# One copy fewer of the attention product, and three steps of the end re-ordered, in a kernel of two gated blocks

## The chip, the cores and the metric

The kernel runs on one core of one Trainium2 chip. The metric is the device time of one execution in microseconds (us). The profile shows one such execution: what each engine did and when. The engines are named as in the profile: PE multiplies matrices, PEld is its weight load, DVE is the vector engine, ACT the scalar engine, POOL the GpSimd engine, and SP issues most DMAs (SPq is its queue).

## The reference

The input x has 4 batches of 1024 rows of 512 numbers. Two layers follow one another. Each normalises x, computes an attention `s` and a feed-forward network `g` from the same normalised x, and adds their gated product:

```
xn = layernorm(x); s = attention0(xn); g = silu(ffn0(xn)); x = x + s * g
xn = layernorm(x); s = attention1(xn); g = silu(ffn1(xn)); x = x + s * g
```

Layer 0 has a linear attention with decay and a ternary-weight FFN; the change does not touch them. Attention 1 is a softmax attention with 16 heads of 32: `q`, `k` and `v` are projections, `q` and `k` are rotated by position, `y = softmax(q k^T / sqrt(32)) v`, and the output is `y wo^T`. FFN 1 has weights in whole numbers from 0 to 63 with the zero point 128 and a scale for each row: `W = (wq - 128) * s`.

## The kernel before

The kernel is one program with five parts in order: attention 0 (to 624 us), FFN 0 (to 1160 us), attention 1 (to 2598 us), FFN 1 (to the end), and a check of FFN 1's weights with a fallback that does not run here. The order of the work on PE is written out by hand. On the other engines a planner chooses the order by its own estimates, except that instructions marked with `keep_in_program_order` (below: pinned) keep the order in which the program names them. Each engine carries out its own queue in order and waits there for what an instruction needs; SP's queue of DMA issues does so too. A tile comes from a pool by its tag, with a fixed number of buffers, and a new tile waits until everyone who read the old one in its buffer is done.

**Units and steps.** Attention 1 is cut into 32 units: batch b (4), group g of four heads (4), and half `qh` of the queries (2), in this order. A unit has 512 queries and 8 key blocks of 128. The loop over `s` (L1177) has 8 steps for a unit, and steps 256 to 268 to finish. Step `s` holds work of several units:

- `top`: the scores `sq` of queries by keys for unit s // 8, of which DVE takes the maxima (L1079). After the eighth step `turn_max` sends the maxima through memory to `mT`.
- `exps(e)` with e = s - 12: scores `sk` of keys by queries (L1105), less the maximum (L1111), and on ACT their exponentials `pT` (L1116, two instructions; three buffers). Exponential e is key block kb = e % 8 of unit e // 8. Then `part` adds up the exponentials over the key blocks: on POOL (L1143 the first addition of a unit, L1145 the others), and on DVE from step 256 on.
- `weigh(e - 1)`: PE adds `v` times `pT` to `y` (L1124). After the last key block ACT copies `y` to `yr` (L1284).
- half a chain of matmuls, where one is waiting: `heads_in` projects q, k and v of a later group (L866; ACT copies to `raw`, DMAs swap rows to `rr`, and POOL rotates in L924 and L925), and `wo_out` multiplies four finished groups with `wo` (L866 too) once the last is divided.

**The division.** The sums over the keys of a unit are taken on DVE: `sums_of` (L967, L972) eight times, two in a step; `gather` (L980 to L984) writes them out and loads them turned, into `sides`, which has the one buffer of the tag that the transposes of `sums_of` use; `invert` (L993, L998) takes the reciprocal, writes it to `inverse_d` (L1001) and loads it spread over the partitions, as `zs` (L1009, four DMAs); `times` (L1017) multiplies `yr` by `zs` on POOL and writes `yT`, which `wo_out` reads. Counted by `i` from the unit's first sums, these are steps 0 to 3, 4, 7 and 10. Unit 30 has steps of its own, written out for the end of the loop; unit 31 is summed on PE and divided in `divide` after it. `yr` has two buffers; `yT` has five for `qh = 0` and six for `qh = 1`.

**Weights.** In steps 244 to 255 SP loads one weight of FFN 1 in each (`weight`, L777, 256 KB, to a tile of the tag `raw`, which has three buffers), and ACT subtracts 128 (L790) one step later, in `loaded()`. Both are pinned. The last two conversions are both named in step 255. The rest of the weights follow in FFN 1.

After the loop PE does the output chains of units 30 and 31 and goes on to FFN 1.

Of the kernel before, what the change touches and what calls it, by code (L numbers as in the profile page):

```python
# [12 lines left out]
F32 = mybir.dt.float32  # L13
# [3 lines left out]
ALU = mybir.AluOpType  # L17
AX = mybir.AxisListType

P = 128  # L20
# [15 lines left out]
def kernel(ctx, tc, ins, out):  # L36
    nc = tc.nc
# [48 lines left out]
    w0 = es1.enter_context(tc.tile_pool(name="w0", bufs=1, reuse_waits="tile"))  # L86
# [159 lines left out]
    with ExitStack() as es:  # L246
# [4 lines left out]
        p2 = es.enter_context(tc.tile_pool(name="a0", bufs=2, reuse_waits="tile"))  # L251
# [273 lines left out]
        for n, (blk, g) in enumerate(steps):  # L525
# [10 lines left out]
            nxt = None  # L536
            if n + 1 < len(steps):
                nxt = project(*steps[n + 1])
# [31 lines left out]
    with ExitStack() as es:  # L570
# [3 lines left out]
        p2 = es.enter_context(tc.tile_pool(name="f0", bufs=2, reuse_waits="tile"))  # L574
# [193 lines left out]
    def weight(stage, pool, pinned=False):  # L768

        m = len(ws)  # L770
        n, c = needed[m]
        q = stage(f"{n}_int{c}").bitcast(I32).rearrange("p (k n) -> p k n", n=P)
        if n == "down":
            src = ins["wq_downT"][c * P : (c + 1) * P, :].rearrange("p (k n) -> p k n", n=P)
        else:
            src = ins[f"wq_{n}T"][:, c * P : (c + 1) * P].rearrange("(k p) n -> p k n", p=P)
        load = nc.sync.dma_start(out=q, in_=src)  # L777
        j = m // 4
        if j not in fours:
            tag = quads[j] if j < len(quads) else f"wf{j}"  # L780
            fours[j] = pool.tile([P, KD, D], F32, tag=tag, name=f"wf{j}")
        w = ws[n, c] = fours[j][:, m % 4, :].bitcast(F32R).rearrange("p (k n) -> p k n", n=P)
        if pinned:
            tc.keep_in_program_order(load)

        def less():
            if pinned:

                tc.keep_in_program_order(
                    nc.scalar.activation(w, q, AF.Identity, bias=less128)  # L790
                )
            else:
                nc.vector.tensor_scalar(w, q, -128.0, None, ALU.add)

        return less
# [19 lines left out]
    with ExitStack() as es:  # L815
# [9 lines left out]
        TB = N // P  # L825
# [187 lines left out]

        def times(u, yr):
            b, g, qh = units[u]
            yT = p2.tile([P, 512], F32, tag=f"yT{qh}", name=f"yT_{b}_{g}_{qh}", bufs=5 + qh)
            tc.keep_in_program_order(nc.gpsimd.tensor_tensor(yT, yr, zss.pop(u), ALU.mult))  # L1017
            yTs[b][g, qh] = yT

        def divide(u, yr, z):  # L1020

            b, g, qh = u
            zs = p2.tile([P, 512], F32, tag="mT", name=f"zs_{b}_{g}_{qh}")
            nc.scalar.copy(zs, z)
            yT = p2.tile([P, 512], F32, tag=f"yT{qh}", name=f"yT_{b}_{g}_{qh}", bufs=5 + qh)
            for c in range(TPB):
                cols = slice(c * P, (c + 1) * P)
                nc.vector.reciprocal(zs[:, cols], zs[:, cols])
            nc.gpsimd.tensor_tensor(yT, yr, zs, ALU.mult)
            yTs[b][g, qh] = yT  # L1030

        def wo_out(b, qh, yT, bank):
            def chain(i):
# [92 lines left out]
                    start=(kb == 0), stop=(kb == TB - 1),  # L1126
                )

        loaded = None

        def exps(e):
            if not 0 <= e < TB * nu:
# [44 lines left out]
        for s in range(TB * nu + LAG + 1):  # L1177

            e = s - LAG
            if s % (2 * TB) == 0 and s < TB * nu:

                assert not must
                n = s // (2 * TB) + 1
                if n < 4 * B:
                    b, g = divmod(n, 4)

                    two = (nc.sync, nc.gpsimd) if s == 0 else (nc.sync, nc.sync)  # L1190
                    must.extend(
                        heads_in(
                            b, g, acc1, {(w, h): two for w in ("wk", "wq") for h in range(2)}
                        )
                    )
                    if g == 3 and b + 1 < B:
                        load1(b + 1)

                left = 2 if n < 4 * B else TB
            if s in soon and s < TB * nu:  # L1200
                spare.extend(wo_out(*soon.pop(s), acc1))
            if s % 2 == 0:

                chain = None
                if spare and left and s < TB * nu:
                    chain = spare.popleft()
                    left -= 1
                elif must:
                    chain = must.popleft()
            if s == 2 * TB:  # L1210
                W["wo"] = shared_tile("wo", "wo")
                tc.keep_in_program_order(
                    nc.sync.dma_start(
                        out=W["wo"], in_=ins["woT"].rearrange("(k p) n -> p k n", p=P)
                    )
                )
            if s % 4 == 0 and s // 4 < TPB:
                lates[s + 2] = s // 4, late(s // 4)
            if s < TB * nu:
                u, j = divmod(s, TB)  # L1220
                if j == 0:
                    mx[u] = p2.tile([P, TPB, 4, 2], F32, tag="mx", name=f"mx_{u}")
                for pair in range(2):
                    top(u, j, pair, mx[u])
                if j == TB - 1:
                    m2 = twice[u % 2][:, :, :8].rearrange("p q (h c) -> p q h c", c=2)

                    w = p2.tile([P, TPB, 4, 2], F32, tag="m1", name=f"m1_{u}")
                    nc.vector.tensor_reduce(
                        w[:, :, :, 0], mx.pop(u), AX.X, ALU.max, negate=True  # L1230
                    )
                    for out, sign in ((w[:, :, :, 1], -1.0), (m2[:, :, :, 0], 1.0)):
                        nc.scalar.activation(
                            out.bitcast(F32R), w[:, :, :, 0], AF.Copy, scale=sign
                        )
                    nc.vector.tensor_reduce(m2[:, :, :, 1], w, AX.X, ALU.add)

            zu, at = divmod(s - 3 * TB, TB)
            for u, i in ((zu - 1, at + TB), (zu, at)):
                if 0 <= u < nu - 2:  # L1240
                    if i < 4:
                        for c in (2 * i, 2 * i + 1):
                            sums_of(u, parts[u], c)
                        if i == 3:
                            parts.pop(u)
                    elif i == 4:
                        gather(u)
                    elif i == 7:
                        invert(u)
                    elif i == 10:  # L1250
                        times(u, ys.pop(u))
                        b, g, qh = units[u]
                        if g == 3:
                            soon[s + 2] = b, qh, yTs[b]

            u = nu - 2
            if s == TB * nu + 7:
                for c in range(8):
                    sums_of(u, parts[u], c)
                parts.pop(u)  # L1260
            elif s == TB * nu + 8:
                gather(u)
            elif s == TB * nu + 10:
                invert(u)
            elif s == TB * nu + LAG:
                times(u, ys.pop(u))
                soon[s] = units[u][0], units[u][2], yTs[B - 1]
            late_exp = s >= TB * nu
            if late_exp:
                exps(e)  # L1270
            if 1 <= e <= TB * nu:
                u, kb = divmod(e - 1, TB)
                if kb == 0:
                    ys[u] = pp.tile([P, 512], F32, tag="y", name=f"y_{u}")
                weigh(u, kb, pTs[e - 1], ys[u])
                if u == nu - 1 and kb < TB // 2:

                    if kb == 0:
                        z_last = acc1(f"z_{u}")
                    total(z_last, pTs[e - 1], kb, TB)  # L1280
                pTs.pop(e - 2, None)
                if kb == TB - 1:
                    yr = p2.tile([P, 512], F32, tag="yr", name=f"yr_{u}")
                    nc.scalar.copy(yr, ys[u])  # L1284
                    ys[u] = yr
            held = 0
            if s % TB == 0 and 0 < s <= TB * nu:
                turn_max(s // TB - 1)
            if s in lates:
                late_turn(*lates.pop(s))  # L1290
            else:
                held = 1
                advance(1)
            if not late_exp:
                exps(e)
            advance(4 - held)
            if TB * nu - 12 <= s < TB * nu:

                nxt = weight(raw1, w0, True)
                if loaded:  # L1300
                    loaded()
                loaded = nxt
                if s == TB * nu - 1:
                    loaded()

        soon = [*soon.values()]
        for new in soon:
# [306 lines left out]
```

## Time and profile before

| | |
|---|---|
| time, median of 3 runs | 3091.44 us (3087.67, 3091.44, 3104.02) |
| the profiled execution | 3092.4 us, of which the span of its instructions is 3090.6 us |
| mean granted TensorE clock | 0.992 |
| busy, share of the span | PE 98%, PEld 56%, DVE 62%, POOL 51%, ACT 37% |
| attention 1 (1160.6 to 2598.3 us) | PE 1411.0, POOL 1171.0, DVE 923.7, ACT 597.8 us busy of 1437.7 |
| last FFN (2598.3 us to the end) | PE 479.1 us busy of 492.3 |
| exponentials, L1116 | 512 instructions, 1021 ns each |
| additions to `part` on POOL, L1145 and L1143 | 182 of 4545 ns and 31 of 4538 ns |
| copy of y, L1284 (ACT) | 32 of 585 ns |
| product with the reciprocal, L1017 (POOL) | 31, median 1272 ns |

The busy times count matmuls from their start to a modelled end, so a busy PE may still be held up. A wait is shown as the idle time before an instruction together with the instruction that ended it, as far as the semaphores show it. PEclk is the granted TensorE clock, 1.00 at full speed. In a step with projections PE needs 5.2 to 5.8 us, without them 4.6 us, as the starts of the y matmuls (L1124) in the timeline show.

### The profile page before, as it was taken

Reading aid. Unit: us, or ns where it says so; the run is one execution under the profiler, and the core shown is the slowest. Engines: PE = TensorE matmul, PEld = TensorE weight load, DVE = VectorE, ACT = ScalarE, POOL = GpSimd, SP = SyncE. Lnnn points to the kernel's source line nnn. Section 1 sums busy time; section 2 is a strip of 40 time slices with the busy share of each in tenths; the row PEclk is TensorE's granted clock in tenths of the full one; section 3 lists DMA queues with packets and bytes.
Section 4 is the critical chain, followed back from the end, with each engine's and each line's share of the span. In section 5 each row is a group of like instructions: output and inputs, shape, how many; then the busy total and the mean of one; then the engine's idle time right before and its main releaser. Section 6 shows DMA issues by size and latency. Waiting matters only on the chain.

```text
span 3090.6 us, 61333 instructions
## 1 busy us (share of the span) xinstructions
PE 3029.4 (98%) x25681; PEld 1725.8 (56%) x25681; DVE 1931.0 (62%) x3038; ACT 1155.4 (37%) x1677; POOL 1570.5 (51%) x745
## 2 busy tenths in 40 slices
PE   9999999999999998999999999999999999999998
PEld 5555555578778873333334444433344425888886
DVE  4444555467777776576666666666666665566655
ACT  3111111145556542444444444444444453333332
POOL 1221212234444444888898988988898960001001
PEclk9999999999999998999999999999999999999999
DMA  4232222323223231010001000010000114222111
GB/s 137 86 86 86 86 86 72 127 96 100 95 92 109 96 129 52 10 45 17 18 21 47 23 21 22 21 52 23 23 20 24 26 55 152 89 69 75 59 52 56
DMA packets 131150, 197.25 MB, mean 64 GB/s; under 512 B 33200, under 2 KB 47024, under 8 KB 130736
## 3 DMA queue, kind: packets, MB, share of 16 engines
q1 hardware_dynamic: 123456, 171.72, 18.7%
q0 software_dynamic: 7280, 21.39, 1.9%
q8 instruction: 203, 3.33, 0.5%
q14 instruction: 83, 0.68, 0.1%
q10 hardware_dynamic: 128, 0.13, 0.0%
HBM read 124.25 MB, written 60.53 MB: 60 GB/s over the span
## 4 chain that ended last, share of the span: by engine, by line
PE 54%; POOL 2%; ACT 1%; SPq 1%; issue 1%; DMA 1%; DVE 1%; POOLq 0%; ACTq 0%; DVEq 0%
PE sk L1105 9%; PE sq L1075 8%; PE y L1124 7%; PE gate L1347 5%; PE up L1347 5%; PE dn L1369 5%; PE wo L866 4%; PE wk L866 3%; PE v1ps L866 3%; PE wq L866 3%; PE sk L1111 2%; ACT pT L1116 1%; POOL part L1145 1%; SPq L920 1%; POOL rr L924 0%
## 5 line engine op out<-in xcount | busy, mean ns | idle before, releaser
L1145 POOL TENSOR_TENSOR part<-part,pT 128x2048 f32<-128x2048 f32 x182 | 827.2, 4545 | 31.2 <-ACT pT L1116 23.3
L1079 DVE TENSOR_REDUCE mx<-sq 128x2 f32<-128x1024 f32 x512 | 605.4, 1219 | 367.8 <-PE sq L1075 367.3
L1116 ACT ACTIVATE pT<-sk 128x1024 f32<-128x1024 f32 x512 | 495.9, 1021 | 610.4 <-PE sk L1111 592.7
L1075 PE MATMUL sq<-wkT,wqT 32*128 32x512 f32 x2048 | 331.0, 642 | 13.9 <-ACT pT L1116 11.2
L1105 PE MATMUL sk<-wqT,wkT 32*128 32x512 f32 x2048 | 332.5, 649 | 4.1 <-ACT pT L1116 3.7
L1124 PE MATMUL y<-pT,v 128*32 128x512 f32 x2048 | 278.7, 615 | 0.1
L1391 POOL TENSOR_TENSOR th<-th,x 128x512 f32<-128x512 f32 x31 | 40.1, 1293 | 458.0 <-DVE th L1390 379.0
L646 PE MATMUL pj<-wpj,hp 128*128 128x512 f32 x1024 | 262.3, 395 | 3.8 <-DVE hp L606 3.8
L593 PE MATMUL fc<-xp,wfc 128*128 128x512 f32 x1024 | 259.0, 395 | 3.6 <-ACT h L598 2.9
L614 POOL TENSOR_TENSOR sums<-sums,h 128x512 f32<-128x512 f32 x112 | 160.6, 1434 | 197.8 <-ACT h L598 192.6
L1111 PE MATMUL sk<-mT,onesr 2*128 2x512 f32 x1024 | 244.5, 799 | 0.0
L382 PE MATMUL qk<-xnT,wqkv 128*128 128x512 f32 x512 | 228.7, 599 | 0.7 <-ACT xnT L156 0.7
L646 PEld LDWEIGHTS pj<-wpj,hp 128*128 128x128 f32 x1024 | 190.8, 188 | 52.5 <-DVE hp L606 11.1
L593 PEld LDWEIGHTS fc<-xp,wfc 128*128 128x128 f32 x1024 | 189.2, 188 | 47.5 <-ACT h L598 6.1
L606 DVE TENSOR_TENSOR hp<-h,hp 128x512 fp32r<-128x512 f32 x128 | 129.2, 1009 | 85.6 <-ACT hp L603 85.6
L1105 PEld LDWEIGHTS sk<-wqT,wkT 32*128 32x128 f32 x2048 | 100.0, 185 | 134.4 <-issue 106.6
L1347 PE MATMUL gate<-xp,wf 128*128 128x512 f32 x704 | 174.1, 389 | 0.0
L1347 PE MATMUL up<-xp,wf 128*128 128x512 f32 x704 | 173.9, 389 | 0.0
L1369 PE MATMUL dn<-wf,hp 128*128 128x512 f32 x704 | 173.5, 389 | 0.0
L1143 POOL TENSOR_TENSOR part<-pT,pT 128x2048 f32<-128x2048 f32 x31 | 140.7, 4538 | 63.7 <-ACT pT L1116 63.6
L1075 PEld LDWEIGHTS sq<-wkT,wqT 32*128 32x128 f32 x2048 | 93.0, 184 | 132.9 <-issue 42.7
L382 PEld LDWEIGHTS qk<-xnT,wqkv 128*128 128x128 f32 x512 | 94.8, 190 | 112.0 <-issue 103.5
(236 smaller groups left out, 4454.6 us busy)
## 6 DMA issues: line engine op xcount, KB each, us to landing
s<-s SPq DMA_DIRECT2D x96, 256.0 KB
xp<-xp_d SPq DMA_DIRECT2D x16, 1024.0 KB
x<-x SPq DMA_DIRECT2D x36, 256.0 KB
x<-in_x SPq DMA_DIRECT2D x32, 256.0 KB
raw_fc<-in_w_fcT SPq DMA_DIRECT2D x32, 256.0 KB
xp_d<-hi POOLq DMA_DIRECT2D x32, 256.0 KB, 2.7
xp_d<-xnT POOLq DMA_DIRECT2D x32, 256.0 KB, 2.9
x0r<-in_x SPq DMA_DIRECT2D x32, 256.0 KB
```

The costliest lines, as they stand in the source:

```text
L382: nc.tensor.matmul(a, lhsT=wqkv[k][:, c0 : c0 + P], rhs=xnTs[blk][:, k, :], start=(k == 0), stop=(k == KD - 1),)
L593: nc.tensor.matmul(a, lhsT=wfc[k][:, c * P : (c + 1) * P], rhs=xp[n][:, k, :].bitcast(F32R), start=(k == 0 and n == 0), stop=(k == KD - 1 ...
L646: nc.tensor.matmul(ds[i], lhsT=hparts[blk, c][n][:, i * P : (i + 1) * P], rhs=wpj[c], start=(c == 0 and n == 0), stop=(c == NH0 - 1 and n ...
L866: nc.tensor.matmul(out[r0 : r0 + HD, :], lhsT=lhsT[:, r0 : r0 + HD], rhs=rhs, start=start, stop=stop,)
L1075: nc.tensor.matmul(sq[:, hh, :], lhsT=qT[r, q0 : q0 + P], rhs=kT[r, n * 512 : (n + 1) * 512], start=True, stop=True,)
L1079: nc.vector.tensor_reduce(mx[:, qt, 2 * pair : 2 * pair + 2, n], sq, AX.X, ALU.max)
L1105: nc.tensor.matmul(sks[h // 2][:, h % 2, :], lhsT=kT[r, kb * P : (kb + 1) * P], rhs=qT[r, qh * 512 : (qh + 1) * 512], start=True, stop=False,)
L1116: nc.scalar.activation(pT[:, 2 * pair : 2 * pair + 2, :], sks[pair], AF.Exp, scale=QKS)
L1124: nc.tensor.matmul(y[r, :], lhsT=v[:, kb, r], rhs=pT[:, h, :], start=(kb == 0), stop=(kb == TB - 1),)
L1145: add.tensor_tensor(parts[u], parts[u], pT, ALU.add)
L1347: nc.tensor.matmul(a, lhsT=ws[n, c][:, k, :], rhs=xp[m][:, k, :], start=(k == 0 and m == 0), stop=(k == KD - 1 and m == 1),)
L1369: nc.tensor.matmul(ds[i], lhsT=hparts[blk, c][n][:, i * P : (i + 1) * P], rhs=w, start=(c == 0 and n == 0), stop=(c == NH1 - 1 and n == 1),)
```

## The change

- ACT's copy of `y` goes straight to a tile of the tag `yT0` or `yT1`, and `times` (for the last unit `divide`) multiplies it in place. The tag `yr` goes; `yT0` and `yT1` have one buffer more each. The tiles in all stay thirteen.
- A weight is converted two steps behind its load: in steps 246 to 257, no longer in 245 to 255.
- The inverse of unit 29 is named at i = 6, no longer 7 (step 262). The sums, the gathering, the inverse and the product of unit 30 are named in steps 262, 263, 265 and 267, each one sooner.

```diff
         def times(u, yr):
             b, g, qh = units[u]
-            yT = p2.tile([P, 512], F32, tag=f"yT{qh}", name=f"yT_{b}_{g}_{qh}", bufs=5 + qh)
-            tc.keep_in_program_order(nc.gpsimd.tensor_tensor(yT, yr, zss.pop(u), ALU.mult))
-            yTs[b][g, qh] = yT
+            tc.keep_in_program_order(nc.gpsimd.tensor_tensor(yr, yr, zss.pop(u), ALU.mult))
+            yTs[b][g, qh] = yr
...
-            yT = p2.tile([P, 512], F32, tag=f"yT{qh}", name=f"yT_{b}_{g}_{qh}", bufs=5 + qh)
...
-            nc.gpsimd.tensor_tensor(yT, yr, zs, ALU.mult)
-            yTs[b][g, qh] = yT
+            nc.gpsimd.tensor_tensor(yr, yr, zs, ALU.mult)
+            yTs[b][g, qh] = yr
...
-        loaded = None
+        loaded = deque()
...
-                    elif i == 7:
+                    elif i == (7 if u < nu - 3 else 6):
                         invert(u)
...
             u = nu - 2
-            if s == TB * nu + 7:
+            if s == TB * nu + 6:
                 for c in range(8):
                     sums_of(u, parts[u], c)
                 parts.pop(u)
-            elif s == TB * nu + 8:
+            elif s == TB * nu + 7:
                 gather(u)
-            elif s == TB * nu + 10:
+            elif s == TB * nu + 9:
                 invert(u)
-            elif s == TB * nu + LAG:
+            elif s == TB * nu + 11:
                 times(u, ys.pop(u))
...
                 if kb == TB - 1:
-                    yr = p2.tile([P, 512], F32, tag="yr", name=f"yr_{u}")
+
+                    qh = units[u][2]
+                    yr = p2.tile([P, 512], F32, tag=f"yT{qh}", name=f"yT_{u}", bufs=6 + qh)
                     nc.scalar.copy(yr, ys[u])
                     ys[u] = yr
...
             if TB * nu - 12 <= s < TB * nu:
 
-                nxt = weight(raw1, w0, True)
-                if loaded:
-                    loaded()
-                loaded = nxt
-                if s == TB * nu - 1:
-                    loaded()
+                loaded.append(weight(raw1, w0, True))
+            if len(loaded) > 2 or loaded and s >= TB * nu:
+
+                loaded.popleft()()
```

## The prediction

> **What bounds the kernel now.** I read the page first, then the busy time by stretches, the waits of PE and of ACT between 1160 and 2598 us (the attention of layer 1, all that the change touches), and at last the timeline of single engines around each wait. PE is busy 3029.4 of 3090.6 us, and 1411 of this stage's 1437.7 us, so an edit pays only where PE stands still or runs at half clock. The waits in the stage:
>
> ```profile
> PE 3029.4 (98%) x25681; PEld 1725.8 (56%) x25681; DVE 1931.0 (62%) x3038; ACT 1155.4 (37%) x1677; POOL 1570.5 (51%) x745
> ...
> PE sq L1075 <- ACT pT L1116: 11.2, 27, 1.9
> PE sk L1105 <- ACT pT L1116: 3.7, 2, 3.4
> PE wo L866 <- POOL yT L1017: 2.1, 1, 2.1
> ...
> ACT yr L1284 <- POOL yT L1017: 39.8, 11, 4.9
> ...
> ACT wf L790 <- DMA up_int<-in_wq_upT: 7.8, 2, 4.2
> ```
>
> (us in all, times, longest.) PE waits for late exponentials, and two things make ACT late: the copy of y into `yr`, which waits for POOL's multiplication two units earlier (two buffers), and twice the conversion of a weight that has not landed. Here is the first conversion in ACT's timeline (start, busy, engine, line; in brackets the idle time before and what ended it):
>
> ```profile
> 2493.80 0.72 ACT L790 ACTIVATE wf<-up_int,less 128x512 fp32r<-128x512 int32 x1 [3.59 <-DMA up_int<-in_wq_upT]
> 2494.43 1.92 ACT L1116 ACTIVATE pT<-sk 128x1024 f32<-128x1024 f32 x2
> ...
> 2501.96 1.94 ACT L1116 ACTIVATE pT<-sk 128x1024 f32<-128x1024 f32 x2 [5.00 <-PE sk L1111]
> ```
>
> and in SP's:
>
> ```profile
> 2485.46 0.39 SPq L1001 DMA_DIRECT2D inverse_d<-inv  x1
> ...
> 2488.61 1.74 SPq L1009 DMA_DIRECT2D zs<-inverse_d  x4
> ...
> 2490.86 0.43 SPq L777 DMA_DIRECT2D up_int<-in_wq_upT  x1
> ```
>
> The load stood behind the four `zs` loads, which wait for `inverse_d` to be written; ACT, in order, held the next exponentials behind the conversion. The last sums, on DVE:
>
> ```profile
> 2536.13 2.29 DVE L1145 TENSOR_TENSOR part<-part,pT 128x2048 f32<-128x2048 f32 x1 [2.21 <-ACT pT L1116]
> ...
> 2561.66 2.29 DVE L1143 TENSOR_TENSOR part<-pT,pT 128x2048 f32<-128x2048 f32 x1 [3.25 <-ACT pT L1116]
> 2563.87 0.58 DVE L993 TENSOR_REDUCE inv<-sides 32x64 f32<-32x256 f32 x1
> ```
>
> The chain that ended last runs through DVE's inverse at 2563.87, the DMAs, POOL's product (2570.88) and PE's output matmuls at 2572.20, and then stays on PE into the last FFN (2598.30). What arrives sooner at 2572.20 moves the end of the kernel by as much.
>
> **The clock.** A window in which K=32 matmuls leave PE partly idle is followed by half clock (columns: window, PE, PEld, DVE, ACT, POOL busy, PEclk, DMA):
>
> ```profile
> 1471.17:1474.58 3.41, 2.48 (x16) 0.76 (x16) 1.51 (x3) 2.43 (x3) 3.41 (x2) 1.00 0.09 19
> 1474.58:1478.00 3.42, 3.42 (x20) 1.07 (x14) 1.05 (x1) 0.00 (x0) 3.34 (x2) 0.50 0.02 5
> 2164.08:2167.49 3.41, 2.74 (x32) 0.95 (x28) 1.23 (x1) 2.43 (x3) 3.41 (x2) 1.00 0.13 25
> 2167.49:2170.91 3.42, 3.42 (x65) 1.83 (x67) 1.23 (x1) 0.64 (x1) 3.34 (x2) 1.00 0.04 10
> ```
>
> Busy 73% brought half clock, 80% with projection matmuls between did not. The Trainium skill ("TensorE: Matmul & The Clock Gate", Part 1) has the clock halved after an idle window of some 3.4 us; the trace speaks against it, since 0.93 us of PE idle sufficed at 1473. By that rule the half clock at 1474 would not go with its stall, and the sum below would be 1.9 us smaller.
>
> **1. Conversions two steps behind.** Nothing is added: twelve loads and twelve conversions (0.72 us on ACT) as before. Number the exponentials by step, unit x 8 + kb. At load 3, exponential 237 could have started at its scores' start plus 1.46 us (that lag is 1733.17 to 1734.63 in an undisturbed step): 2491.40 + 1.46 = 2492.86. It started at 2494.43. Half clock held from 2495.2 to 2502.0, and exponential 238, due 4.59 us later (the step without projections) at 2497.45, came at 2501.96: 4.5 us lost. Moved, the conversion stands behind exponential 237, which ends at 2494.8; the load landed by 2493.8, so 1.0 us covers it. If that cover goes, the old stall returns. A load now finds its buffer (three) free one step later; what stands behind it on SP is the gathering of sums and the `mT` loads, and these have 18 us (issued by 2492.6, first scores of unit 30 near 2511), so I price that wait at nothing.
>
> The second stall (4.22 us of ACT at 2529.3 to 2533.55, load 11) is worth less than its 3.4 us of PE idle and 6.8 us of half clock, because the DVE sums are next in line: from the end of POOL's last addition (2531.59) DVE needs 4 additions x 2.29 and 4 pairs of sums x 0.93 before the gathering at 2546.22, and waited only 2.21 for an exponential. Gain: 2.2. Bounds: 0 (load 11 can again be awaited: by my rows it lands near 2529, 1.8 us after exponential 245 would end) to 5.5, should PE be what is late.
>
> **2. Last sums one step sooner.** Same instructions: eight transposes and reductions, one gathering, one inverse, one product, each a step sooner. The sums of unit 30 (from 2550.77) already start right behind the inverse of unit 29, which starts when its DMA lands (2549.67), so their move alone gives 0; nothing else is queued behind that inverse on DVE, nor behind its DMAs on SP or the product on POOL. The inverse of unit 30 does gain: `sides` took 3.21 us after the gathering of unit 29 (2546.46 to 2549.67), so here it was there at 2558.42 + 3.21 = 2561.63; the inverse started at 2563.87 behind the addition. Gain 2.2. Now it waits ahead of that addition: the last three additions of unit 31 (6.9 us) slip by up to 3, and their reader, PE's total at 2576.72, comes 7 us after the last of them (2569.57): covered.
>
> Steps 1 and 2 add along one chain: 4.5 + 2.2 + 2.2 = 8.9 us at 2572.20. PE's wait there grows from 2.1 to near 3, among K=128 matmuls (its window was 44% busy and stayed at full clock). Price if it is halved: 1.7 to 3.4.
>
> **3. `yr` gone.** Thirteen buffers as before (6 + 7 for 5 + 6 + 2), the multiplication stays 1.27 us, the copy 0.58. The copy now needs a slot that output matmuls read last: those of the first `qh=0` group read until 1679.5 and their slot is wanted near 1769.6 (unit 12), `qh=1` until 1854.5, wanted at 1903.8 (unit 15): 49 us of cover, price nothing. What goes is the wait of 39.8 us on ACT. On PE I measure it by the starts of successive y matmuls. Seven times (after units 11, 13, 15, 19, 21, 23, 27) a step takes 6.90 to 7.57 where the same place undisturbed takes 5.80: 1.5, 1.4, 1.1, 1.1, 1.8, 1.4, 1.1, together 9.5 us. But POOL is late there in itself (POOL's timeline, then two lines of ACT's):
>
> ```profile
> 1713.51 1.28 POOL L924 TENSOR_TENSOR rr<-rr,cs 128x512 f32<-128x512 f32 x1 [3.36 <-DMA rr<-raw_wk]
> ...
> 1727.81 1.28 POOL L1017 TENSOR_TENSOR yT<-yr,zs 128x512 f32<-128x512 f32 x1
> ...
> 1740.72 4.54 POOL L1143 TENSOR_TENSOR part<-pT,pT 128x2048 f32<-128x2048 f32 x1
> ...
> 1729.12 0.58 ACT L1284 COPY yr<-y 128x512 f32<-128x512 f32 x1 [4.64 <-POOL yT L1017]
> ...
> 1745.29 1.94 ACT L1116 ACTIVATE pT<-sk 128x1024 f32<-128x1024 f32 x2
> ```
>
> From 1713.51 to 1745.25 POOL has no gap over 0.08, and exponential 99 starts 0.03 after the addition that frees its `pT` (three buffers); the same 0.03 recurs in all seven. PE 1.5 us ahead meets that addition instead. An exponential can be some 0.4 late at no cost (a copy late by d costs d - 2.0, the exponential is then late by d - 1.6), and 0.1 of it is used, so PE keeps 0.3: 7 x 0.3 = 2 us. Bounds: 0 (POOL's order binds fully) to 9.5 (POOL takes the first addition ahead of the `rr` pair, 2.5 us).
>
> After unit 5 POOL binds less: the step took 5.62 against 4.82 after unit 1, and the next, at half clock, 6.51 against 4.59: 2.7. After units 3 and 7 another 0.1 and 0.3. Together 3; bounds 1.1 (half clock stays) to 3.1.
>
> **The sum.** 8.9 + 2 + 3 = 13.9. The profiled execution took 3092.4 us (span 3090.6 and 1.8 around it), 1.0 above the median of 3091.4. From the median: 3091.4 - 13.9 = 3077.5, say 3078.
>
> **Rivals.** *The whole `yr` wait is won* (POOL reorders): 8.9 + 9.5 + 3 = 21.4, 3070. For: POOL's order between pinned products is a planner's. Against: its inputs arrive as before.
> *A load still holds ACT, or the late idle halves the clock*: the new order puts the last conversion behind exponential 245, in steps of 2.4 us; ACT may place an unpinned exponential ahead or behind, as it did with 244. The 2.2 of the second stall goes and 3.4 of half clock comes: 13.9 - 5.6 = 8.3, 3083. If the planner undoes the shift for load 3 too, 4.5 more: 3088. That is also the case of a change that doesn't do what it says.
> *Slower*: each of the seven moved waits (exponential kb=3) leaves a window less than about three quarters busy, and two windows at half clock cost 3.4 each: 7 x 3.4 - 13.9 = +10, 3101. It decides between 73% and 80% busy. Against: at the old place windows as low as 80% stayed at full clock, and the moved waits are shorter (1.2 of 1.5).
>
> **Chances.** Forecast 0.5, whole `yr` wait 0.17, partly lost 0.23, slower 0.1. About 0.5% (15.5 us) is what a measurement of this kernel tells from no change: 3076.0 and 3106.9 are the bounds. The forecast lies 2 us short of the first, so about a third of its 0.5 counts as faster, with all of the second case and a little of spread (the three runs lie 16 us apart): faster 0.37. A part of the slower case passes the upper bound, with a re-planned order that I don't see: slower 0.09. The rest is 0.54. The range takes in the whole `yr` wait with 4 us of spread, and the undone shift: 3066 to 3091.
>
> **What would show it.** Right: no wait of ACT's copy for POOL, exponential 238 4.6 us after 237, no half clock near 1474 and 2495, DVE's inverse of unit 30 within 3.3 us of its gathering, PE's output matmuls near 2558, and in seven units an exponential kb=3 that waits for POOL. Wrong: steps of 5.80 in the seven places with 5.25 at kb=3 (the larger gain), a conversion that still waits for DMA, half clock at a new place, or waits of ACT for PE's output matmuls.

## The result

The kernel after takes 3081.04 us (median of 20 runs, 3076.76 to 3091.23); the kernel before, run in the same sessions, 3093.38 us (20 runs, 3087.67 to 3109.06). The ratio is 0.9959 [0.9947, 0.997], a gain of 12.3 us where 13.9 were forecast and 3078 us was given. The profiled executions lie 8.6 us apart: 3083.8 us (span 3082.0) against 3092.4.

Executions of one kernel also differ ahead of unit 1: it began at 1262.4 us here, at 1263.4 in before, and at 1251.6 in an experiment that changes nothing ahead of it (the copy alone). Before spends 20.5 us at half clock between 1164 and 1229; that execution spends none there. So all traces are compared below by the shift of a place against before, counted from the start of unit 1 (its first y matmul, L1122, which was L1124 before). For the kernel after that is:

| first y matmul of | unit 7 | 11 | 29 | 30 | 31 | last step | end of output matmuls | end of the FFN |
|---|---|---|---|---|---|---|---|---|
| shift, us | -2.2 | -2.5 | -2.6 | -7.1 | -11.0 | -7.6 | -7.6 | -7.6 |

The trace thus gives the change 7.6 us; another 1.0 lies ahead of unit 1 and is not its work. The medians give 3.7 more than the profiles, since the profiled execution of after lies 2.8 above its median and that of before 1.0 below; the interval of the medians begins at 9.3 us (0.3%). No trace shows a median execution, but each run comes with its mean granted clock. Over 83 runs of the kernel before, timed beside the experiments, the time rises by some 3.1 us for each 0.001 that the mean clock falls (correlation -0.92). The 20 runs of after have 0.9944 in the mean and their profiled execution 0.993, which is enough for its 2.8 us. Those 83 have 0.9925, so by the same slope an estimated 6 us of the gain of the medians are less half clock. The page's line of the engines, after:

```profile
PE 3024.9 (98%) x25681; PEld 1728.5 (56%) x25681; DVE 1931.3 (63%) x3038; ACT 1156.5 (38%) x1677; POOL 1572.4 (51%) x745
```

And the waits of PE and of ACT in it (1160 to 2600 us):

```profile
PE sq L1073 <- ACT pT L1114: 6.8, 20, 0.8
PE y L1122 <- ACT pT L1114: 3.5, 1, 3.5
...
ACT yT L1284 <- PE y L1122: 33.6, 31, 2.0
ACT pT L1114 <- POOL part L1143: 32.8, 9, 4.3
...
ACT pT L1114 <- POOL part L1141: 8.6, 7, 1.3
...
ACT pT L1114 <- DVE part L1141: 4.0, 1, 4.0
```

The copy of y waits for PE alone; the 39.8 us behind POOL's product are gone. In their place exponentials wait for POOL's additions, 41.4 us in all, which is what the prediction had set against a whole gain. New is one wait of 4.0 for an addition on DVE, with PE's 3.5 behind it. ACT's timeline has the two conversions and this wait:

```profile
2489.25 1.94 ACT L1114 ACTIVATE pT<-sk 128x1024 f32<-128x1024 f32 x2 [2.05 <-PE sk L1109]
2491.10 0.72 ACT L790 ACTIVATE wf<-up_int,less 128x512 fp32r<-128x512 int32 x1
2493.84 1.94 ACT L1114 ACTIVATE pT<-sk 128x1024 f32<-128x1024 f32 x2 [2.03 <-PE sk L1109]
...
2525.35 0.72 ACT L790 ACTIVATE wf<-up_int,less 128x512 fp32r<-128x512 int32 x1 [1.70 <-DMA up_int<-in_wq_upT]
...
2555.89 1.94 ACT L1114 ACTIVATE pT<-sk 128x1024 f32<-128x1024 f32 x2 [3.96 <-DVE part L1141]
```

At 2491.10 the conversion of load 3 lies in an idle stretch, behind its exponential and without a wait. The last load still holds ACT for 1.70 us. The last line is the last exponential, 255. It writes into the buffer of exponential 252 (`pT` has three), and that is free when the first addition of unit 31 has read it. DVE's timeline shows why that is late:

```profile
2548.92 0.24 DVE L980 STREAM_TRANSPOSE back<-groups 128x64 f32<-128x64 f32 x1
2552.47 0.60 DVE L993 TENSOR_REDUCE inv<-sides 32x64 f32<-32x256 f32 x1 [3.30 <-DMA sides<-groups_d]
2553.11 0.54 DVE L998 RECIPROCAL inv<-inv 32x64 f32<-32x64 f32 x1
2553.58 2.22 DVE L1141 TENSOR_TENSOR part<-pT,pT 128x2048 f32<-128x2048 f32 x1
```

The inverse of unit 30, moved ahead, stands idle for 3.30 us until `sides` lands, and the addition stands behind it. The windows of the clock (window, busy PE, PEld, DVE, ACT, POOL, PEclk, DMA, GB/s):

```profile
1473.73:1477.14 3.41, 2.59 (x20) 0.93 (x16) 1.29 (x2) 1.72 (x2) 3.33 (x2) 1.00 0.00 0
2525.04:2528.45 3.41, 2.57 (x20) 0.91 (x20) 3.31 (x2) 2.77 (x4) 1.91 (x1) 1.00 0.01 3
2528.45:2531.86 3.41, 3.41 (x20) 0.91 (x17) 3.31 (x6) 1.72 (x2) 0.00 (x0) 0.50 0.00 0
2552.35:2555.76 3.41, 1.07 (x12) 0.16 (x8) 3.25 (x3) 0.00 (x0) 0.00 (x0) 1.00 0.02 2
2555.76:2559.17 3.41, 2.21 (x12) 0.69 (x16) 3.20 (x3) 1.94 (x2) 0.37 (x1) 0.50 0.25 82
```

(Where the rotation is moved in the kernel after, these lines are L1132 for y, L1124 for exponentials, and L1151 and L1153 for the additions.) No half clock is left near 1474 and 2495. One window of it follows the last load, and two (to 2562.6) follow the late exponential. The shifts add up so: 2.6 up to unit 29, 4.5 in it, 3.9 in unit 30, and 3.4 given back between the start of unit 31 and its last step.

### The profile page after: what moved, and what is told of

Its sections match the earlier page's. It is cut to its first block, busy times and chain, and to the rows that moved or that the text cites. A ratio compares the mean times of both kernels' runs of the same rounds, so it can differ in the third digit from the quotient of the medians.

```text
span 3082.0 us, 61307 instructions
## 1 busy us (share of the span) xinstructions
PE 3024.9 (98%) x25681; PEld 1728.5 (56%) x25681; DVE 1931.3 (63%) x3038; ACT 1156.5 (38%) x1677; POOL 1572.4 (51%) x745
## 4 chain that ended last, share of the span: by engine, by line
PE 53%; POOL 3%; issue 1%; DVE 1%; ACT 1%; SPq 0%; DMA 0%; POOLq 0%; ACTq 0%; DVEq 0%
PE sk L1103 8%; PE sq L1073 8%; PE y L1122 7%; PE gate L1345 5%; PE up L1345 5%; PE dn L1367 5%; PE wo L866 4%; PE wk L866 3%; PE wq L866 3%; PE v1ps L866 3%; PE sk L1109 2%; POOL part L1143 2%; ACT pT L1114 1%; POOL part L1141 0%; POOL rr L924 0%
## 5 line engine op out<-in xcount | busy, mean ns | idle before, releaser
L1073 PE MATMUL sq<-wkT,wqT 32*128 32x512 f32 x2048 | 331.3, 640 | 10.4 <-ACT pT L1114 6.8
L1122 PE MATMUL y<-pT,v 128*32 128x512 f32 x2048 | 277.1, 612 | 3.6 <-ACT pT L1114 3.5
```

The costliest lines, as they stand in the source:

```text
L1073: nc.tensor.matmul(sq[:, hh, :], lhsT=qT[r, q0 : q0 + P], rhs=kT[r, n * 512 : (n + 1) * 512], start=True, stop=True,)
L1122: nc.tensor.matmul(y[r, :], lhsT=v[:, kb, r], rhs=pT[:, h, :], start=(kb == 0), stop=(kb == TB - 1),)
```

## The experiments

The first three make one part of the change each in the kernel before; the others say which kernel they edit. Where intervals overlap, a verdict rests on the traces, and so on one execution of each kernel. Shifts are counted as above.

**The copy alone.** The first part of the diff, nothing else:

```diff
-            yT = p2.tile([P, 512], F32, tag=f"yT{qh}", name=f"yT_{b}_{g}_{qh}", bufs=5 + qh)
-            tc.keep_in_program_order(nc.gpsimd.tensor_tensor(yT, yr, zss.pop(u), ALU.mult))
+            tc.keep_in_program_order(nc.gpsimd.tensor_tensor(yr, yr, zss.pop(u), ALU.mult))
...
-                    yr = p2.tile([P, 512], F32, tag="yr", name=f"yr_{u}")
+                    yr = p2.tile([P, 512], F32, tag=f"yT{qh}", name=f"yT_{u}", bufs=6 + qh)
```

> The first part alone: the copy of y goes to yT and the product is taken in place; conversions and last sums as before. Theory (POOL's run binds): ACT's copy waits for POOL no more, the half clock after unit 5 goes, and in the seven odd units the step of 6.90 to 7.57 us falls to 5.80, but the step with kb=2 of the next unit grows from 5.25 to about 6.4; 2.2 us won at units 5 and 6, 0.3 after units 3 and 7, about 0 in the seven: 2.5 us faster than before. Rival (the buffer was the whole cause): the seven steps stay won, 9.5 + 2.5 = 12 us faster.

Measured: 3087.12 us, ratio 0.9993 [0.9974, 1.0011]; shift at unit 29 -3.5, at the end of the output matmuls -0.9, at the end of the FFN -0.1. The waits of ACT in it (1213 to 2560 us):

```profile
ACT pT L1114 <- POOL part L1143: 32.0, 9, 4.1
...
ACT pT L1114 <- POOL part L1141: 8.6, 7, 1.3
ACT wf L790 <- DMA up_int<-in_wq_upT: 8.5, 2, 4.4
```

The seven steps of 6.90 to 7.57 are all 5.80 now, but in the units that follow them the step of kb = 2 takes 6.38 to 6.45 in place of 5.25, and three of kb = 0 take 0.3 to 0.4 more. It adds up to nothing. What is won is the place after unit 5: 5.62 and 6.51 became 4.82 and 4.81. The loads still hold ACT (8.5 us, 7.8 before). Of the 3.0 us that are left at the last step, 2.1 go in the output matmuls: PE's wait for POOL's last product is 2.50 there, in a window 27% busy (2555.15), and half clock follows at 2558.6. That is the price of 1.7 to 3.4 that the prediction had set on a longer wait at this place.

**The conversions alone.** The second part:

```diff
-                nxt = weight(raw1, w0, True)
-                if loaded:
-                    loaded()
-                loaded = nxt
...
+                loaded.append(weight(raw1, w0, True))
+            if len(loaded) > 2 or loaded and s >= TB * nu:
+                loaded.popleft()()
```

> The second part alone: weights are converted two steps behind their loads. Theory (the conversions are behind most of the gain): the step of 7.08 us in unit 29 and its neighbour of 6.60 fall to 4.6, 4.5 us; the last load is still awaited for about 1.7 us, so the second place gives 1 to 2 us; 5.5 to 6.5 us faster than before. Rival (the waits are hidden by what comes after, in the DVE sums): under 2 us faster.

Measured: 3080.14 us, 0.9966 [0.9948, 0.9984]; shift -0.5 at unit 29, -5.0 at unit 30, -7.4 at unit 31, -7.0 at the end. Unit 29's steps of 7.08 and 6.60 are 4.59 and 4.59: 4.50 us, as predicted, against the same trace from which the prediction read the loss. At the second stall unit 30 has 2.45, 5.77 and 3.94 and a window at half clock (2523.9): the shift grows there by 2.4 us.

**The last sums alone.** The third part:

```diff
-                    elif i == 7:
+                    elif i == (7 if u < nu - 3 else 6):
...
-            if s == TB * nu + 7:
+            if s == TB * nu + 6:
...
-            elif s == TB * nu + 10:
+            elif s == TB * nu + 9:
```

> The third part alone: the sums, the gathering, the inverse and the product of unit 30 one step sooner. Theory A (of the changed kernel's trace): the inverse, now ahead of DVE's addition for exponential 253, ends 2.2 us sooner, but the addition comes behind it, and exponential 255 waits for that addition (it frees its buffer), some 0.6 us longer than before; PE's output matmuls win 1 to 1.5 us. Theory B (of the prediction): 2.2 us won and nothing else late.

Measured: 3084.12 us, 0.9989 [0.9973, 1.0006]. From unit 31 to the end of the output matmuls the shift goes from -2.4 to -3.6: 1.2 us of the 2.2; the last step takes 1.83 in place of 1.15. The -2.9 in unit 29 is none of its doing. The first load held ACT here as long as in before:

```profile
2488.04 0.72 ACT L790 ACTIVATE wf<-up_int,less 128x512 fp32r<-128x512 int32 x1 [3.63 <-DMA up_int<-in_wq_upT]
```

But no half clock followed it, and the two steps took 6.18 and 4.59 in place of 7.08 and 6.60. So this stall costs 1.6 us without half clock and 4.5 with it.

**POOL's rotation later, in the kernel after.** If the order of POOL binds at the seven places, taking the `rr` pair (the second half of q's rotation) out from ahead of the first addition must give the 9.5 us that taking the copy away did not.

```diff
-                nc.gpsimd.tensor_tensor(rr, rr, cs[:, 1, cols], ALU.mult)
-                nc.gpsimd.tensor_tensor(dst[:, cols], dst[:, cols], rr, ALU.add)
+                def rotate():
+                    yield nc.gpsimd.tensor_tensor(rr, rr, cs[:, 1, cols], ALU.mult)
+                    yield nc.gpsimd.tensor_tensor(dst[:, cols], dst[:, cols], rr, ALU.add)
+                if n == "wq" and half and (b or g > 1):
+                    rotates.append((now, rotate))
+                else:
+                    for _ in rotate():
+                        pass
...
                         times(u, ys.pop(u))
+                        while rotates and rotates[0][0] <= s:
+                            for op in rotates.popleft()[1]():
+                                tc.keep_in_program_order(op)
```

> The changed kernel with POOL's rotation of the second half of q (two instructions, 2.5 us) moved behind the next product with the reciprocal, so that the first addition of the next unit comes 2.5 us sooner. Theory (POOL's run binds at kb=3): the seven steps of 6.35 to 6.45 us fall to 5.25, 8 us faster than the changed kernel, some 20 us faster than before. Rival (something else than POOL, ACT or DVE, sets that step): no more than 2 us faster than the changed kernel.

Measured: 3072.34 us, 0.9944 [0.9925, 0.9964]; from unit 11 to unit 29 the shift goes from -3.0 to -11.9, 8.9 us, and to -19.0 at the end. POOL and ACT at the first of the seven places, first in the kernel after, then in this one:

```profile
1734.79 1.28 POOL L924 TENSOR_TENSOR rr<-rr,cs 128x512 f32<-128x512 f32 x1
1737.38 4.54 POOL L1141 TENSOR_TENSOR part<-pT,pT 128x2048 f32<-128x2048 f32 x1
...
1730.25 1.94 ACT L1114 ACTIVATE pT<-sk 128x1024 f32<-128x1024 f32 x2 [4.11 <-POOL part L1143]
1741.95 1.94 ACT L1114 ACTIVATE pT<-sk 128x1024 f32<-128x1024 f32 x2 [1.27 <-POOL part L1141]
```

```profile
1734.65 4.55 POOL L1151 TENSOR_TENSOR part<-pT,pT 128x2048 f32<-128x2048 f32 x1
...
1730.12 1.94 ACT L1124 ACTIVATE pT<-sk 128x1024 f32<-128x1024 f32 x2 [4.08 <-POOL part L1153]
1740.45 1.92 ACT L1124 ACTIVATE pT<-sk 128x1024 f32<-128x1024 f32 x2
```

With the `rr` pair gone from ahead of it the first addition starts 2.7 us sooner, and the exponential that reuses its buffer no longer waits for it. All seven steps of kb = 2 are 5.25 again. The load at the end still brings half clock (2518.8, 6.8 us; a step of 6.75 in unit 30).

**The same rotation in the kernel before.** Does it need the change at all?

> The kernel before with the same later rotation on POOL, and none of the change. Theory (two waits in a row, the buffer first and POOL's additions behind it): the copy still waits for the product of two units earlier, which keeps its place in POOL's queue, so the seven steps of 6.9 to 7.6 us stay and the time is that of before within 1 us. Rival (POOL's run was the whole cause, and the buffer none): the seven steps fall to 5.80, 9 us faster.

Measured: 3090.76 us, 0.9994 [0.9977, 1.0011]; the seven steps stay at 6.97 to 7.77, and the shift from unit 11 to 29 is +0.7. (After unit 5, in contrast, it is enough: 5.62 and 6.51 become 4.82 and 4.87 here, and the shift at unit 7 is -2.3, where the copy alone has -2.6. At the end of the output matmuls nothing is left of it, +0.1.) The copy to `yr` still waits, as ACT's waits (1160 to 2600 us) show:

```profile
ACT yr L1298 <- POOL yT L1027: 32.9, 8, 5.1
```

Two waits stood one behind the other, for the `yr` buffer and for POOL's first addition. From unit 11 to 29, taking away the first alone gives 0.6 us (the copy alone), the second alone nothing, both 8.9.

**The inverse of unit 30 at its old step, in the kernel after.** This undoes the one move that brought DVE's late addition.

```diff
-            elif s == TB * nu + 9:
+            elif s == TB * nu + 10:
                 invert(u)
```

> The changed kernel with the inverse of unit 30 named a step later again (266), behind DVE's addition for exponential 253; its sums, gathering and product stay sooner. Theory (the inverse, waiting for its DMA, held that addition, and the addition the buffer of exponential 255): exponential 255 waits no more, its y step falls from 4.6 us to about 2.4, the inverse starts no later than before the edit; PE then waits some 3 us for the product of unit 30; the output matmuls end 0 to 2 us sooner, or up to 1.5 us later if half clock follows that wait. Rival (exponential 255 is late for another reason): the step stays at 4.6.

Measured: 3084.01 us, 0.9963 [0.9949, 0.9978]; shift -13.5 at unit 31, -13.1 at the last step, -8.9 at the end. The wait of the last exponential is gone (PE 0.50), since the first addition runs ahead of the inverse, but now PE runs out of work. DVE's and PE's timelines:

```profile
2545.00 2.25 DVE L1141 TENSOR_TENSOR part<-pT,pT 128x2048 f32<-128x2048 f32 x1
2548.31 0.59 DVE L993 TENSOR_REDUCE inv<-sides 32x64 f32<-32x256 f32 x1 [1.06 <-DMA sides<-groups_d]
...
2548.42 1.54 PE L1122 MATMUL y<-pT,v 128*32 128x512 f32 x6 [0.50 <-ACT pT L1114]
...
2557.73 6.02 PE L866 MATMUL wo<-wo,yT 128*32 128x256 f32 x80 [4.75 <-POOL yT L1016]
```

Two windows of it:

```profile
2554.00:2557.41 3.41, 0.00 (x0) 0.00 (x0) 0.02 (x1) 0.00 (x0) 1.00 (x1) 1.00 0.32 72
2557.41:2560.83 3.42, 3.10 (x32) 1.50 (x36) 0.00 (x0) 0.58 (x1) 0.26 (x1) 0.50 0.00 0
```

At the last step the old place of the inverse is 5.5 us ahead of the kernel after, at the end of the output matmuls 1.3: PE stands idle for 4.75 us and then has half the clock for 3.4. Of the 5.5, 2.5 were there at unit 31 already, ahead of the inverse: the last load held ACT as in the kernel after, but no half clock followed. The fair comparison is the run with the last two conversions later (below), which has the inverse moved and about the same lead at unit 31 (-13.7) and ends at -7.4. By these two traces the inverse's move, priced at a gain of 2.2, costs 1.5; the medians, 3084.01 against 3084.16 and 3081.04 for the kernel after, with overlapping intervals, don't show it.

**Ready output matmuls into that gap.** The kernel of the last experiment, with six of eight parts of the first three output chains, whose inputs are ready, named ahead.

```diff
+        ahead = [*spare][:3]
+        for chain in ahead:
+            advance(6)
         for m, chain in enumerate(spare):
-            advance(8)
+            advance(2 if m < 3 else 8)
```

> As the run before, and PE does the first three quarters of three output chains of unit 30 before the last quarter of the first, which is what waits for the product (8 us of work in place of 2.7). Theory (the end of the stage is the wait for that product): PE no longer stands still there, no half clock follows, and the output matmuls end about 5 us sooner than in the changed kernel. Rival (PE is bound there by its own work or by ACT's copies out of PSUM): under 2 us.

Measured: 3076.96 us, 0.995 [0.9928, 0.9971]; shift -12.5 at the last step, -14.7 at the end, no half clock after 1207 us until the last 11 us of the span. PE runs through:

```profile
2547.13 1.54 PE L1122 MATMUL y<-pT,v 128*32 128x512 f32 x6 [0.69 <-ACT pT L1114]
...
2548.51 10.11 PE L866 MATMUL wo<-wo,yT 128*32 128x256 f32 x172
```

**The last two conversions two steps later, in the kernel after.** It asks what the last load's wait and its half clock cost.

```diff
-            if len(loaded) > 2 or loaded and s >= TB * nu:
+            if len(loaded) > 2 or loaded and s >= TB * nu + 2:
```

> The changed kernel with the last two conversions two steps later still (258 and 259). Theory (ACT still waits about 1.7 us for the last load, and half clock follows): no conversion waits for a DMA, the steps of 4.26 and 3.94 us in unit 30 fall to 2.4 and 3.2, no half clock there; but DVE's additions and sums come next, so the inverse of unit 30 comes only 0.5 to 1.5 us sooner, and the time falls by that. Rival (what PE lost there counts in full): 3 us or more.

Measured: 3084.16 us, 0.9971 [0.9959, 0.9983]; shift -13.7 at unit 31 (after: -11.0), -7.1 at the last step, -7.4 at the end (after: -7.6). ACT:

```profile
2528.11 0.74 ACT L790 ACTIVATE wf<-up_int,less 128x512 fp32r<-128x512 int32 x1
...
2532.92 1.94 ACT L1114 ACTIVATE pT<-sk 128x1024 f32<-128x1024 f32 x2 [1.52 <-DVE part L1143]
2536.86 1.94 ACT L1114 ACTIVATE pT<-sk 128x1024 f32<-128x1024 f32 x2 [2.00 <-DVE part L1143]
...
2555.61 1.94 ACT L1114 ACTIVATE pT<-sk 128x1024 f32<-128x1024 f32 x2 [5.64 <-DVE part L1141]
```

The load's wait and its half clock are gone and unit 31 begins 2.7 us sooner, and all of it is spent in waits for DVE: two exponentials now wait for its additions of unit 30, and the first two steps of unit 31 take 3.84 and 3.94 in place of 3.16; the last exponential waits 5.64 for 3.96 for the addition behind the inverse. In the kernel after, the second stall costs the end nothing.

**Rotation, old inverse and outputs ahead together**, in the kernel after.

> The changed kernel with the later rotation, the inverse of unit 30 where it was, and three output chains ahead. Theory (the two waits left by the change are apart from each other, one in POOL's run and one at the end): the gains add, 9 us in the odd units and 7 at the end, 14 to 18 us faster than the changed kernel and 25 to 28 faster than before. Rival (the end of the stage takes back what the middle wins, since DVE's and POOL's sums set it): no faster than the run with the later rotation alone, some 19 us faster than before.

Measured: 3072.4 us, 0.9924 [0.9906, 0.9942]; shift -10.4 at unit 29, -16.2 at unit 31, -18.5 at the end. The middle holds its 8.4 us (unit 11 to 29), but the last load is awaited again and two windows at half clock (from 2521.0) stretch unit 30: steps of 6.06 and 4.31.

**All four**: the same with the last two conversions two steps later.

> The run before with the last two conversions in steps 258 and 259 as well. Alone that edit moved the end of the stage by 0.2 us, since the product of unit 30 was what PE waited for. Theory (with three output chains ahead PE's own path sets the end, so what ACT lost to the last load now counts): no conversion waits for a DMA, the two long steps of unit 30 (6.06 and 4.31 us) fall to 2.4, its half clock goes, and the output matmuls end 4 to 7 us sooner than in the run before; some 28 us faster than before the change. Rival (DVE's sums still set it): within 1.5 us of the run before.

Measured: 3065.6 us (median of 6 runs, 3062.0 to 3071.11), 0.9906 [0.989, 0.9923]: faster than both kernels, with an interval apart from that of the kernel after. Shift -11.4 at unit 29, -23.0 at unit 31, -23.1 at the end. The waits of ACT:

```profile
ACT pT L1124 <- POOL part L1153: 26.9, 7, 4.1
...
ACT pT L1124 <- DVE part L1153: 3.5, 2, 2.0
```

No conversion waits, and attention 1 has no half clock after 1206 us. The edit that gave nothing in the kernel after is worth 3.6 us here: the end is 4.6 sooner (-23.1 against -18.5), and 1.0 of that was there at unit 29, ahead of it. That fits the account that the tail had swallowed it, by one execution of each.

## Why the prediction was right, and where its steps were not

The time came out within the range and near the figure. By the trace the steps earned it only in part: 7.6 us of 13.9 in that execution, with one step that gave nothing, and a loss that was declared covered. That is nearer to the 8.3 of the rival with a late load; that the median came so near to 13.9 is in part luck, of the clock by the estimate above. One sign did not come: the output matmuls that need the product of unit 30 began at 2563.4 us, not near 2558, and PE's wait for that product is not among its waits any more. It was done at 2561.71, and PE was late itself.

**Conversions, first stall: 4.5 forecast, 4.50 measured**, in the kernel after as in the part alone. The mechanism (an exponential in order behind a load, then two windows at half clock) held. The size is that of the one execution from which it was read and against which it is measured: with the old conversions, the same two steps lost 5.2 us in the copy alone, 4.3 with the rotation moved in the kernel before, and 1.6 in the last sums alone; 6.8, 3.4 and 0 us of half clock followed there, 6.8 in before.

**Conversions, second stall: 2.2 forecast, 1.2 measured** on the chain for which it was priced. The gathering of unit 29 went from 2546.22 to 2536.90, 8.3 us after taking off the 1.0 ahead of unit 1, and unit 30 had begun 7.1 sooner. The warning that load 11 may be awaited came true: 1.70 us instead of 4.22, and half clock from 2528.4. What cost the rest is a term that the sum did not have. POOL's product now delays DVE's second addition, which in before came only after it (2536.13, behind an exponential). DVE's and POOL's timelines, after:

```profile
2523.53 5.57 DVE L1143 TENSOR_TENSOR part<-part,pT 128x2048 f32<-128x2048 f32 x2 [2.40 <-POOL part L1143]
...
2524.16 2.79 POOL L1016 TENSOR_TENSOR yT<-yT,zs 128x512 f32<-128x512 f32 x1 [0.66 <-PE sk L1109]
...
2558.80 2.91 POOL L1016 TENSOR_TENSOR yT<-yT,zs 128x512 f32<-128x512 f32 x1 [10.88 <-DMA zs<-inverse_d]
```

Two additions take 5.57 where two alone take 4.6, and the product 2.79 instead of 1.28. They take turns: the first addition ends at 2525.83, the product 1.12 later at 2526.95, the second addition (shown from 2525.93) 2.15 after that, at 2529.10. DVE has no gap from there to the gathering, so these 1.0 us are the rest. The trace of before had such a pair to read it from: there the product of unit 28 met the first addition (2531.62), and only the product was held up:

```profile
2532.15 2.89 POOL L1017 TENSOR_TENSOR yT<-yr,zs 128x512 f32<-128x512 f32 x1 [0.56 <-DMA zs<-inverse_d]
```

The same delays the product of unit 30 at 2558.80 beside the additions that the change put there. The Trainium skill ("SBUF — State Buffer", Who interferes with whom) says that a DVE instruction with two SBUF inputs contends with a GpSimd instruction that reads SBUF, and that this is an exclusive lock; these ends agree with it.

**Last sums: 2.2 forecast, 2.1 measured at the inverse, and 3.4 given back.** The inverse of unit 30 came at 2552.47, 10.4 us sooner (again less the 1.0) against 8.3 for its gathering. But the step had named as the only reader of the three additions PE's total, 7 us after them, and said: covered. It left out the buffers that an addition sets free. Exponential 255 waits for them too, through the three `pT`; it waited 3.96 us, PE 3.55, and 6.8 us of half clock followed. The price that the prediction held ready for half clock in the tail (1.7 to 3.4) is the one that came, by another door than the wait for POOL's product. The experiments show that moving the inverse back removes this wait and opens the one for POOL's product, and that ready matmuls fill that one.

**Seven places of `yr`: 2 forecast, nothing measured.** That POOL binds behind the copy was right, and with it the forecast against a whole gain. The wait of the exponential kb = 3 in all seven units shows it, and so does the experiment with the rotation, which delivered 8.9 of the 9.5. Wrong was the 0.3 us that PE was to keep at each. The steps lost 9.5 us in before and lose 9.6 now, against undisturbed ones: seven of kb = 2 by 1.1 to 1.2 and three of kb = 0 (units 12, 14, 22) by 0.4 to 0.6. The lag that an exponential can have at no cost was counted as a gain at each place, and none of it shows. I read the result so that POOL's run without gaps sets the rate over a pair of units, and what is gained inside it is waited for again; that reading was not tested by itself. The three late steps of kb = 0 are POOL's too. In all seven units an exponential waits there for POOL's addition, 3.57 to 3.61 us where the step is not late, 4.11, 4.22 and 4.29 in units 12, 14 and 22. ACT in units 14 and 16:

```profile
1817.99 1.94 ACT L1114 ACTIVATE pT<-sk 128x1024 f32<-128x1024 f32 x2 [4.22 <-POOL part L1143]
...
1905.13 1.94 ACT L1114 ACTIVATE pT<-sk 128x1024 f32<-128x1024 f32 x2 [3.61 <-POOL part L1143]
```

With the rotation moved the three waits are 4.08, 3.92 and 3.82, and the steps are late by 0.4, 0.2 and 0.1. Why POOL is later in just these three stays open.

**After unit 5, and after units 3 and 7: 2.7 and 0.4 forecast, 2.2 and 0.3 measured.** The step after unit 5 is 4.82, the next 5.10 at full clock, as the window behind that of 1473.73 has it (PEclk 1.00); against the 4.59 forecast, 0.5 us went into waits for POOL's additions.

**The rivals.** The slower one did not come: seven moved waits, and no half clock in any of them. The one with a late load came in its second half, wait and half clock; but the experiment that took both away gained nothing at the end, so it priced a place where the end was not decided.

## What to carry to other kernels

Behind a wait on an in-order engine stands the next one. Before pricing it, find the second limit at the same place, and price the two as a pair: here a copy's buffer and POOL's order gave 0.6 us and nothing apart and 8.9 us together, and one and the same edit gave nothing or 3.6 with a different tail behind it. And a loss read from one trace is the loss of that execution: the same stall cost 1.6 to 5.2 us, by the half clock that followed. When an instruction that waits is moved ahead on its engine, the readers to look up are all of what it delays: those of the outputs, and also the writers that wait for a buffer which it should set free.

## What was not expected of the hardware

- DVE's additions and POOL's products hold each other up by whole instructions: 2.29 us became 3.17, and 1.28 became 2.79 to 2.91 (2.89 in before).
- Half clock is not tied to one share of busy time. Where score matmuls (K=32) run with some of y among them, it followed windows 73% busy (1471.17 before) and 75% (2525.04 after), but not one of 75% (2529.31 before) or of 72% (2519.87 with the inverse at its old step). By this share alone it can't be forecast.
- Among matmuls over all 128 rows (y and output) it followed windows 0% (2554.00, old inverse), 27% (2555.15, copy alone) and 31% busy (2552.35 after), and not one of 44% (2570.27 before). The Trainium skill ("TensorE: Matmul & The Clock Gate", Part 1: The HAM clock gate) puts half clock behind an idle window of some 3.4 us; the first of these agrees with it, the other two had matmuls in them all the same.
